# Layer 0 of a four-layer network: how projections are dealt out over attention units, and where small statistics products are written

## The chip, the cores and the metric

The kernel runs on one core of one Trainium2 chip. The time is the device time of one execution in microseconds (us). The core has five engines that run side by side and wait for each other through semaphores: TensorE (PE in the profile, with its weight loads as PEld), VectorE (DVE), ScalarE (ACT), GpSimd (POOL) and SyncE (SP), which here issues nearly all transfers. Everything is computed in 32-bit floats.

## The reference, cut to what matters

Four images of 56 x 56 pixels with 256 channels pass through four layers. Each layer adds something to its input, and normalises its input by groups of 8 channels first:

```python
def _gn(v, G=32, eps=1e-5):                     # per image: mean and variance of each group of 8 channels
    g = v.reshape(B_, H_, W_, G, C_ // G)
    m = jnp.mean(g, axis=(1, 2, 4), keepdims=True)
    s = jnp.var(g, axis=(1, 2, 4), keepdims=True)
    return ((g - m) / jnp.sqrt(s + eps)).reshape(v.shape)

x = x + _L0_conv_ref(_gn(x), ...)               # local attention, 7 x 7 window, 8 heads of 32
x = x + _L1_conv_ref(_gn(x), ...)               # a graph product over the tokens of each image
x = x + _L2_conv_ref(_gn(x), ...)               # neighbourhood attention, 7 x 7, half of the heads dilated by 2
x = x + _L3_conv_ref(_gn(x), ...)               # attention within shifted 7 x 7 windows

def _L0_conv_ref(x, wq, bq, wk, bk, wv, bv, wo, bo):
    q = x @ wq.T + bq; k = x @ wk.T + bk; v = x @ wv.T + bv
    ...                                         # to 8 heads of 32 channels
    k_unf = _unfold(k); v_unf = _unfold(v)      # the 49 neighbours of each pixel, zeros outside the image
    logits = jnp.einsum('ndhw,ndkhw->nkhw', q, k_unf) * scale
    attn = jax.nn.softmax(logits, axis=1)
    out = jnp.einsum('nkhw,ndkhw->ndhw', attn, v_unf)
    ...
    return out @ wo.T + bo
```

The statistics of an image must be complete before the first of its pixels can be normalised. That is what ties the steps around this change together.

## The kernel before, in words

**Units of layer 0.** An image is cut into 8 blocks of 7 rows (`NB0`), and a block into 4 columns (`NTC`) that are 16, 12, 12 and 16 pixels wide. A block and a column make a unit: 32 blocks, 128 units, numbered here through all images. The columns at the sides are wide units (112 queries), the inner ones narrow (84). `pair(r, t)` describes unit t of block r. For each unit there are

- *logits* (L1067): products of queries and keys into two double banks `ps_s`. VectorE adds a mask to the first half (L1074), after which ScalarE takes exp (L1075). ScalarE takes exp of the second half at once (L1077), and GpSimd multiplies that by a mask (L1078);
- *both* (L1087): GpSimd adds pairs of the exps;
- *products* (L1096): the exps times the values and times ones, into one bank `ps_o` (two buffers), the output bank. They fill 448 or 336 of its 512 columns;
- *finish*: VectorE adds a count of outside pixels (L1246), takes the reciprocal (L1249, or L1244 for inner units) and multiplies (L1251), into `attn`. ScalarE reads the reciprocals once for a check (L998).

`attend_pairs` sets the order of the trace: logits of unit u, then the *fill* of unit u, then products and finish of unit u - 1. The fill is a list of other steps, and this is what the change deals out anew.

**What goes into the fills.** An image's input is also cut into 7 chunks of 8 rows (`NCH`). For each chunk, `prepare` has ScalarE normalise it (L942) into `xn`, and `project_rows` makes six steps: values twice (`value_tiles`, L979, drained by VectorE at L983 and stored to DRAM), keys twice and queries twice (`project`, L952, drained by ScalarE at L1202 and L1211). All write banks of `ps_m`, of which there are two. `project_out` makes two steps for the block before (L952 with `w_wo`, drained by VectorE at L1275 into `xr`). `first_look` has VectorE take the statistics of a chunk of the next image (L896), and `load` fetches such a chunk.

**Statistics.** When the last part of an image's statistics is there, `add_stats` appends three steps to `pending`: `channels` (VectorE, L910), `mean` (a product with a group matrix, L914, read by ScalarE at L916 and L917) and `scale` (two products, L921 and L922, read by ScalarE at L923, then small steps on GpSimd from L924 to L928). The products write 2 columns of a whole `ps_m` bank. `step_stats` does the next pending step; `known` does all that is left when somebody needs the result.

**Who sets the order.** `stream` in `layer0` builds each block's list of steps and `spread` cuts it into four equal parts by the number of entries, whatever an entry is. The list holds projection steps, `prepare` as an entry of its own, looks, one entry with loads, the output steps in the middle and, in blocks 0 and 4 to 7 of each image, three `step_stats`. Block r takes projection entries up to `(7 * (7 * r + 12)) // 8`. From block 29 (`ALONE`) the first steps of layer 1 take the place of projections. In layers 0 and 2 a scheduler may still move an instruction ahead on its engine where its inputs are ready; in layers 1 and 3 some engines keep the written order. Layer 2 has units of the same form (`pair` at L1954), filled from a list that is written out by column, with `step_stats` in the columns 1, 4 and 5 of eight.

Of the kernel before, what the change touches and what calls it, by code (L numbers as in the profile page):

```python
# [40 lines left out]
NCH = 7  # L41
# [19 lines left out]
NB0 = S // TR  # L61
BT = TR * S
COLS = (0, 16, 28, 40, 56)
NTC = 4
# [766 lines left out]
def direct_blocks(ctx: ExitStack, tc: tile.TileContext, d: dict, watch):  # L831
# [40 lines left out]
    def psum_tile(tag, bufs, banks=1):  # L872
        shape = [P, 512] if banks == 1 else [P, banks, 512]
        return ps.tile(shape, FP, tag=tag, name="ps_" + tag, bufs=bufs)
# [3 lines left out]
    def ps_m():  # L878
        return psum_tile("m", m_bufs)
# [6 lines left out]

    parts_of = [NCH, NB0, NCH, 2 * NSB]
    raw = [[const.tile([P, CC, n, 6], FP, name=f"st{l}_{b}") for b in range(NIMG)] for l, n in enumerate(parts_of)]
    stats, pending = {}, []
    seen_parts = {}  # L890

    def add_stats(l, b, i, x):
# [8 lines left out]
    def group_stats(l, b):  # L901

        st = raw[l][b]
        mv = const.tile([P, CC, 2], FP, name=f"mv{l}_{b}")
        gst = const.tile([P, CC, 3], FP, name=f"gst{l}_{b}")
        dv = const.tile([P, CC], FP, name=f"dv{l}_{b}")

        def channels():
            for h in range(CC):
                nc.vector.bn_aggr(out=mv[:, h, :], in_=st[:, h].rearrange("p a b -> p (a b)"))  # L910

        def mean():
            pm = ps_m()
            nc.tensor.matmul(pm[:, :CC], lhsT=group, rhs=mv[:, :, 0], start=True, stop=True)  # L914
            for h in range(CC):
                nc.scalar.activation(dv[:, h:h + 1], pm[:, h:h + 1], AF.Square, bias=mv[:, h, 0:1], scale=-1.0)  # L916
            nc.scalar.copy(gst[:, :, 0], pm[:, :CC])  # L917

        def scale():
            pm = ps_m()  # L920
            nc.tensor.matmul(pm[:, :CC], lhsT=group, rhs=dv, start=True, stop=False)  # L921
            nc.tensor.matmul(pm[:, :CC], lhsT=group, rhs=mv[:, :, 1], start=False, stop=True)  # L922
            nc.scalar.activation(dv, pm[:, :CC], AF.Identity, bias=gn_eps)  # L923
            nc.gpsimd.tensor_tensor(gst[:, :, 1], dv, mhalf, ALU.pow)  # L924
            nc.gpsimd.tensor_tensor(gst[:, :, 2], gst[:, :, 0], gst[:, :, 1], ALU.mult)
            nc.gpsimd.tensor_scalar_mul(gst[:, :, 2], gst[:, :, 2], -1.0)
            w = watch[1][:, :2 * CC].rearrange("p (h a) -> p h a", h=CC)
            nc.gpsimd.tensor_tensor(w, w, gst[:, :, :2], ALU.add)  # L928
            stats[l, b] = gst
        return [channels, mean, scale]  # L930
# [119 lines left out]


    newest = []

    def attend_pairs(pool, units):

# [68 lines left out]
    def lazily(make, i, n):  # L1124

        made = []
        return [lambda k=k: (made or made.extend(make(i)), made[k]()) for k in range(n)]
# [7 lines left out]
    def layer0(early, big, pool, begin_layer1):  # L1135
# [10 lines left out]
        def first_look(r):  # L1146

            with tc.issue_after(newest[0].ins) if newest else nullcontext():
                add_stats(0, *divmod(r, NCH), looks.pop(r))
# [36 lines left out]
        def project_rows(r):  # L1186

            b, g = divmod(r, NCH)
            xn = xns.pop(r)
            at = left(g, CH)  # L1190
            v = brief.tile([P, 4, C], FP, tag="v", name="v0", bufs=1)

            def values(a):
                value_tiles(v, a, g, CH, xn, wv, bv0, vd[b])

            def keys(m):
                pm = project(wk, m * P, lambda h: xn[:, h, at:at + CH], CH)
                rows = pm.rearrange("p (r c) -> p r c", c=S)
                for i in range(NTC):
                    c0, n = key_range(*COLS[i:i + 2])  # L1200
                    dst = (kE if i in (0, NTC - 1) else kI)[:, m, i // 2, 8 * g:8 * (g + 1), :]
                    nc.scalar.activation(dst, rows[:, :, c0:c0 + n], AF.Identity, bias=bk0[:, m:m + 1])  # L1202

            def queries(m):
                pm = project(wq, m * P, lambda h: xn[:, h, at:at + CH], CH)
                y = 8 * g
                while y < 8 * (g + 1):
                    i, y1 = y // TR, min((y // TR + 1) * TR, 8 * (g + 1))
                    if (b, i) not in q:
                        q[b, i] = early.tile([P, CC, BT], FP, tag="q", name="q0", bufs=6)  # L1210
                    nc.scalar.activation(q[b, i][:, m, (y - TR * i) * S:(y1 - TR * i) * S],  # L1211
                                         pm[:, (y - 8 * g) * S:(y1 - 8 * g) * S],
                                         AF.Identity, bias=qbias[:, 0, m:m + 1], scale=SCALE)
                    y = y1

            return [lambda f=f, m=m: f(m) for f in (values, keys, queries) for m in range(2)]

        def pair(r, t):

# [8 lines left out]
            box = {}  # L1228

            def gather():  # L1230
                box["o"] = psum_tile("o", 2)
                box["v"] = pool.tile([P, 2, C], FP, tag="vp", name="vp0", bufs=3)
                src = vd[b][:, :]
                for u, k0 in enumerate((0, second)):
                    for p, y, x, rows, cols in row_runs(k0, nk, n):
                        nc.sync.dma_start(out=box["v"][p:p + rows * cols, u, :], in_=bass.AP(
                            src.tensor, src.offset + ((r0 + y) * S + c0 + x) * C, [[S * C, rows], [C, cols], [1, C]]))
# [43 lines left out]
        def stream():  # L1281
            n = NIMG * NCH
            rows = []
            for c in range(2, n):
                rows += lazily(project_rows, c, 6)
                rows.append(lambda c=c: prepare(c + 1) if c + 1 < n else None)
            look_at = {}
            for b in range(NIMG - 1):
                for i in range(NCH):
                    look_at.setdefault(NB0 * b + min(i // 2 + (b == 0), 3), []).append((b + 1) * NCH + i)  # L1290
            gone = 0
            for r in range(NIMG * NB0):
                b, g = divmod(r, NB0)
                to = min(len(rows), (7 * (7 * r + 12)) // 8)
                steps, gone = rows[gone:to], to
                steps += [lambda i=i: first_look(i) for i in sorted(looks)]
                steps.append(lambda r=r: [load(i, looks, "xs") for i in look_at.get(r + 1, [])])
                if 0 < r < ALONE:
                    at = (len(steps) + 2) // 2
                    steps[at:at] = project_out(r - 1)  # L1300
                if g > 3 or g == 0:
                    size = len(steps) + 3
                    for i in range(3):
                        steps.insert(i * size // NTC, step_stats)
                attns[r] = pool.tile([P, CC, BT], FP, tag="attn", name="attn0")
                if r < ALONE:
                    yield from spread([pair(r, t) for t in range(NTC)], steps)
                    continue
                if r == ALONE:
                    passing.close()  # L1310
                    tokens.extend(begin_layer1())
                out = project_out(r - 1)
                for t in range(NTC):
                    w = pair(r, t)
                    w["fill"] = lambda steps=tokens.pop(0) + (out[t - 1:t] if t else []): [f() for f in steps]
                    yield w
# [10 lines left out]
        attend_pairs(pool, stream())  # L1327
        for step in tokens.pop(0) + project_out(NIMG * NB0 - 1):
            step()

# [519 lines left out]
    def layer2(held, big, pool, brief, last_steps, ends):  # L1852
# [64 lines left out]
        def pair(r, m, i):  # L1917
# [23 lines left out]

            def gather():
                box["o"] = psum_tile("o", 2)
                box["v"] = pool.tile([P, 2, 2, P], FP, tag="vp", name="vp2", bufs=3)
                src = vd[im][:, :]
                for t in range(2):
                    c0 = window_range(*cols[t], n)[0]
                    if m == 0:
                        v0, sr, sc = (r0 * S + c0) * C, S * C, C
                    else:  # L1950
                        v0, sr, sc = ((2 * r0 + a) * S + 2 * c0 + b) * C + P, 2 * S * C, 2 * C
                    for u, k0 in enumerate((0, second)):
                        for p, ky, kx, rows, some in row_runs(k0, nk, nc_):
                            nc.sync.dma_start(out=box["v"][p:p + rows * some, t, u, :], in_=bass.AP(  # L1954
                                src.tensor, src.offset + v0 + ky * sr + kx * sc, [[sr, rows], [sc, some], [1, P]]))
# [83 lines left out]
        attend_pairs(pool, stream())  # L2039
        for step in project_out(NIMG * NSB - 1):  # L2040
            step()

# [370 lines left out]
```

## Time and profile before

| what | value |
|---|---|
| median of 3 runs | 3770.52 us (3767.21 to 3772.34) |
| profiled execution, its own time | 3769.93 us |
| its span, first to last instruction | 3768.0 us |
| instructions | 112324 |
| granted TensorE clock, mean | 0.994 |
| layer 0, first logits to last products | 39.8 to about 735 us |
| layer 1 | about 732 to 2600 us |
| layer 2 | about 2600 to 3250 us |
| layer 3 | to 3768 us |

The stage limits are read from TensorE's instructions in order of time. A line of a group or of the timeline names the source line, the engine, the operation and the tiles it writes and reads; "x16" counts instructions, of which a 32-bit product takes two, so a projection step of keys, queries or output has 16 and one of two value tiles 32. Idle time in brackets stands before the instruction, with the instruction whose end released it. PEclk is the granted TensorE clock as a share of full speed.

### The profile page before, as it was taken

To read this page: it belongs to the slowest core of one execution; us is meant where nothing else is said; L and a number is where in the kernel's file an instruction comes from. 1 tells how busy PE (TensorE), PEld (TensorE's weight loads), DVE (VectorE), ACT (ScalarE), POOL (GpSimd) and SP (SyncE) were. 2 spreads that over 40 slices of the span, in tenths; PEclk is the share of its full clock that TensorE was granted. 3 is DMA by queue.
4 is the path that set the end of the run, shared out by engine and by line. 5 is a ranking of instruction groups with operands and counts; after the bars stand their busy time and mean duration, and the time that the engine had idled before them with its cause. 6 is when DMAs were issued, how large, how long until landed. Compare 5 with 4: busy or idle time off the path is not lost. (4 is left out here: it accounts for less than half of the span.)

```text
span 3768.0 us, 112324 instructions
## 1 busy us (share of the span) xinstructions
PE 3665.8 (97%) x48826; PEld 2478.1 (66%) x48826; DVE 2200.9 (58%) x4188; ACT 1472.2 (39%) x3125; POOL 1815.9 (48%) x1966
## 2 busy tenths in 40 slices
PE   8999999999999999999999999999999999999998
PEld 4555556677776777767777667775666666555554
DVE  5777777634445444464344544445676777777676
ACT  5565566422222222222222222222666666444443
POOL 4777777612235222352222421123777777555555
PEclk9999999999999999999999999999999999999999
DMA  6544444300010000011000000002544444534443
GB/s 213 169 153 134 132 123 137 134 7 23 23 27 29 22 19 18 21 32 28 19 16 22 26 20 10 11 20 78 138 133 137 132 128 119 155 126 139 130 134 99
DMA packets 278039, 304.94 MB, mean 81 GB/s; under 512 B 33624, under 2 KB 268764, under 8 KB 277084
## 3 DMA queue, kind: packets, MB, share of 16 engines
q1 hardware_dynamic: 275680, 297.43, 25.7%
q8 instruction: 385, 6.31, 0.7%
q0 software_dynamic: 1568, 0.16, 0.1%
q14 instruction: 118, 0.97, 0.1%
q10 hardware_dynamic: 288, 0.08, 0.0%
HBM read 205.04 MB, written 92.55 MB: 79 GB/s over the span
## 5 line engine op out<-in xcount | busy, mean ns | idle before, releaser
L1564 DVE TENSOR_TENSOR acc<-acc,ps_v 128x257 f32<-128x257 f32 x1104 | 463.8, 422 | 781.8 <-PE ps_v L1642 753.4
L1642 PE MATMUL ps_v<-xw,e 128*128 128x257 f32 x2208 | 611.0, 381 | 3.4 <-DVE xnT L1509 2.2
L1637 PE MATMUL ps_o<-xw,at 128*128 128x257 f32 x2208 | 609.0, 379 | 0.0
L1532 PE MATMUL ps_s<-xnT,xd 128*128 128x512 f32 (+3 forms) x1344 | 571.4, 548 | 3.9 <-DVE xnT L1509 3.9
L1626 ACT COPY at<-ps_t 128x512 f32<-128x512 f32 (+3 forms) x332 | 170.6, 514 | 960.9 <-PE ps_t L1623 960.7
L1642 PEld LDWEIGHTS ps_v<-xw,e 128*128 128x128 f32 x2208 | 413.4, 189 | 144.6 <-issue 83.2
L1087 POOL TENSOR_TENSOR b<-e 126x336 f32<-126x336 f32 (+5 forms) x512 | 499.5, 997 | 7.7
L1637 PEld LDWEIGHTS ps_o<-xw,at 128*128 128x128 f32 x2208 | 419.1, 190 | 60.1
L952 PE MATMUL ps_m<-xn,w_wqkv 128*32 128x392 f32 x4096 | 376.4, 496 | 8.0 <-ACT gst L917 3.4
L1525 POOL TENSOR_SCALAR xd<-xnT,vec 128x128 f32<-128x128 f32 x192 | 116.4, 616 | 478.0 <-PE ps_s L1532 477.8
L1078 POOL TENSOR_TENSOR e<-e,m0t 126x672 f32<-126x672 f32 (+3 forms) x128 | 238.8, 1865 | 182.1 <-ACT e L1077 180.6
L1535 ACT ACTIVATE e<-ps_s 128x512 f32<-128x512 f32 x336 | 185.4, 552 | 355.0 <-PE ps_s L1532 351.8
L1532 PEld LDWEIGHTS ps_s<-xnT,xd 128*128 128x128 f32 x1344 | 225.4, 191 | 141.4 <-issue 126.2
L1078 POOL TENSOR_TENSOR e<-e,bias 119x784 f32<-119x784 f32 (+5 forms) x128 | 239.4, 1870 | 157.3 <-ACT e L1077 156.9
L1096 PEld LDWEIGHTS ps_o<-e,vp 124*32 124x32 f32 (+3 forms) x8192 | 200.3, 110 | 101.9 <-issue 84.1
L998 ACT ACTIVATE no<-rs 128x168 f32<-128x168 f32 (+2 forms) x256 | 94.0, 367 | 426.0 <-DVE rs L1960 190.2
L952 PEld LDWEIGHTS ps_m<-xn,w_wqkv 128*32 128x32 f32 x4096 | 123.8, 110 | 183.1 <-issue 128.6
L1960 DVE RECIPROCAL rs<-ps_o 128x196 f32<-128x196 f32 (+2 forms) x128 | 175.7, 1372 | 109.7 <-PE ps_o L1096 108.0
L1096 PE MATMUL ps_o<-e,vp 124*32 124x112 f32 (+3 forms) x8192 | 232.2, 249 | 3.1 <-POOL e L1078 2.5
L1075 ACT ACTIVATE e<-e 126x672 f32<-126x672 f32 (+5 forms) x256 | 219.7, 858 | 13.3 <-DVE e L1074 1.9
L1077 ACT ACTIVATE e<-ps_s 126x672 f32<-126x672 f32 (+5 forms) x256 | 206.3, 806 | 5.4 <-PE ps_s L1067 3.0
L979 PE MATMUL ps_m<-w_wqkv,xn 128*32 128x256 f32 x3136 | 196.9, 381 | 2.1 <-DVE v L983 1.6
(214 smaller groups left out, 5945.5 us busy)
## 6 DMA issues: line engine op xcount, KB each, us to landing
x<-xr SPq DMA_DIRECT2D x64, 392.0 KB
x<-in_x SPq DMA_DIRECT2D x53, 448.0 KB
x<-x SPq DMA_DIRECT2D x60, 392.0 KB
xr<-x SPq DMA_DIRECT2D x60, 392.0 KB
vd<-v SPq DMA_DIRECT2D x72, 256.0 KB
xr<-in_x SPq DMA_DIRECT2D x32, 392.0 KB
xr<-x SPq DMA_DIRECT2D x28, 448.0 KB
x<-xr SPq DMA_DIRECT2D x28, 448.0 KB
```

What stands on the lines that cost most here:

```text
L952: nc.tensor.matmul(pm[j * HD:(j + 1) * HD, :n], lhsT=w[:, h, col + j * HD:col + (j + 1) * HD], rhs=rhs(h), start=(h == 0), stop=(h == CC - 1))
L979: nc.tensor.matmul(pm[i:i + HD, j * C:(j + 1) * C], lhsT=xn[:, h, first + i:first + i + HD], rhs=w[:, h, :], start=(h == 0), stop=(h == CC ...
L1075: nc.scalar.activation(ev, ev, AF.Exp)
L1077: nc.scalar.activation(ev, sv, AF.Exp)
L1078: nc.gpsimd.tensor_tensor(parts(ev), parts(ev), w["emask"], ALU.mult)
L1087: nc.gpsimd.tensor_tensor(w["b"][a][:nk, :, :2 * nq].rearrange("p h (i c) -> p h i c", i=2), ev[:, :, :, 0, :], ev[:, :, :, 1, :], ALU.add)
L1096: nc.tensor.matmul(w["o"](k, i)[j * HD:(j + 1) * HD], lhsT=ones[:nk, :HD] if k else v(j, u), rhs=w["b"][j // 2][:nk, j % 2, i * nq:(i + 1) ...
L1532: nc.tensor.matmul(s[:, :n], lhsT=xd[j][:, h, :], rhs=xnT[:, h, first * P:last * P], start=(h == 0), stop=(h == CC - 1))
L1535: nc.scalar.activation(e[:, :n], s[:, :n], AF.Exp, scale=5.0)
L1564: nc.vector.tensor_tensor(acc[:, i, :], acc[:, i, :], pv[:, :C + 1], ALU.add)
L1637: nc.tensor.matmul(out[j][:, :C + 1], lhsT=e[:, col(i)] if i == j else at[:, col(i)], rhs=xw[:, i, :], start=(i == j), stop=(i == NB - 1))
L1642: nc.tensor.matmul(pv[:, :C + 1], lhsT=e[:, col(i)], rhs=xw[:, j, :], start=True, stop=True)
```

## The change

In layer 0, the entries of a block fall into two kinds. Products (projection and output steps) are shared out over the four units by their number alone, in the new generator `balanced`. All other steps are assigned to units by hand (`free`): `step_stats` at the head of units 0, 1 and 2, looks in unit 1 (the first two) and unit 2 (the rest), loads in unit 3. `prepare` is tied to the last projection step of a chunk. Block r takes projection entries up to `(6 * (7 * r + 12)) // 8`, six to a chunk. From the third chunk's list on (r of 2 and more) the six steps come as keys, values, queries for the first half and then for the second. Looks at the next image are loaded three chunks to a block (`i // 3`), so that an image's statistics are complete a block earlier, and `step_stats` stands in block 3 as well.

The products of `mean` and `scale` write columns 508 to 511 of the output bank `ps_o` of the unit in which they are traced, where such a bank is at hand (`spare`, set by `gather` in layers 0 and 2 and cleared after them), instead of a bank of `ps_m`.

```diff
+    stats, pending, spare = {}, [], []
...
         def mean():
-            pm = ps_m()
+            pm = spare[0][:, 508:510] if spare else ps_m()
...
         def scale():
-            pm = ps_m()
+            pm = spare[0][:, 510:512] if spare else ps_m()
...
+    def balanced(units, steps, free):
+
+        n = len(units)
+        for i, w in enumerate(units):
+            mine = free[i] + steps[i * len(steps) // n:(i + 1) * len(steps) // n]
+            w["fill"] = lambda mine=mine: [f() for f in mine]
+            yield w
...
-            return [lambda f=f, m=m: f(m) for f in (values, keys, queries) for m in range(2)]
+            kinds = (keys, values, queries)
+            if r < 2:
+                return [lambda f=f, m=m: f(m) for f in (values, keys, queries) for m in range(2)]
+            return [lambda f=f, m=m: f(m) for m in range(2) for f in kinds]
...
                 box["o"] = psum_tile("o", 2)
+                spare[:] = [box["o"]]
...
-                rows += lazily(project_rows, c, 6)
-                rows.append(lambda c=c: prepare(c + 1) if c + 1 < n else None)
+                *most, last = lazily(project_rows, c, 6)
+                rows += most + [lambda c=c, last=last: (last(), prepare(c + 1) if c + 1 < n else None)]
...
-                    look_at.setdefault(NB0 * b + min(i // 2 + (b == 0), 3), []).append((b + 1) * NCH + i)
+                    look_at.setdefault(NB0 * b + i // 3 + (b == 0), []).append((b + 1) * NCH + i)
...
-                to = min(len(rows), (7 * (7 * r + 12)) // 8)
+                to = min(len(rows), (6 * (7 * r + 12)) // 8)
                 steps, gone = rows[gone:to], to
-                steps += [lambda i=i: first_look(i) for i in sorted(looks)]
-                steps.append(lambda r=r: [load(i, looks, "xs") for i in look_at.get(r + 1, [])])
+                new = [lambda i=i: first_look(i) for i in sorted(looks)]
+                free = [[], new[:2], new[2:], [lambda r=r: [load(i, looks, "xs") for i in look_at.get(r + 1, [])]]]
                 if 0 < r < ALONE:
-                    at = (len(steps) + 2) // 2
+                    at = (len(steps) + 1) // 2
                     steps[at:at] = project_out(r - 1)
-                if g > 3 or g == 0:
-                    size = len(steps) + 3
+                if g > 2 or g == 0:
                     for i in range(3):
-                        steps.insert(i * size // NTC, step_stats)
+                        free[i].insert(0, step_stats)
...
-                    yield from spread([pair(r, t) for t in range(NTC)], steps)
+                    yield from balanced([pair(r, t) for t in range(NTC)], steps, free)
...
         for step in tokens.pop(0) + project_out(NIMG * NB0 - 1):
             step()
+        spare.clear()
```

Layer 2 gets the line with `spare[:]` in its `gather` and the line with `spare.clear()` at its end.

More of the change, by code (lines that the diff above doesn't have):

```diff
@@ L888, in direct_blocks @@
     raw = [[const.tile([P, CC, n, 6], FP, name=f"st{l}_{b}") for b in range(NIMG)] for l, n in enumerate(parts_of)]
-    stats, pending = {}, []
+    stats, pending, spare = {}, [], []
     seen_parts = {}
@@ L1943, in gather @@
                 box["o"] = psum_tile("o", 2)
+                spare[:] = [box["o"]]
                 box["v"] = pool.tile([P, 2, 2, P], FP, tag="vp", name="vp2", bufs=3)
@@ L2041, in layer2 @@
             step()
+        spare.clear()
     def table_steps(big, pool):
```

## The prediction, made before the changed kernel ran

> **What bounds the kernel now.** I read the page first, then stretches of layer 0, then who waited for whom, then the order in time.
>
> ```profile
> PE 3665.8 (97%) x48826; PEld 2478.1 (66%) x48826; DVE 2200.9 (58%) x4188; ACT 1472.2 (39%) x3125; POOL 1815.9 (48%) x1966
> PEclk9999999999999999999999999999999999999999
> ```
>
> TensorE is busy for 3665.8 of 3768.0 us, and both kernels issue the same number of instructions on every engine. So only the 102 us in which TensorE stands, and the slow-clock time, can be won. Layer 0 ends near 735 us. The stretches answer has length, then busy time of TensorE first:
>
> ```profile
> 60.00:500.00 440.00, 415.00 (x9469) 257.17 (x9465) 324.38 (x472) 259.45 (x617) 323.02 (x268) 0.99 0.46 144
> 500.00:629.00 129.00, 128.48 (x3076) 81.56 (x3068) 99.49 (x141) 80.71 (x187) 104.47 (x82) 1.00 0.40 125
> ```
>
> The first stands for 25.0 us, the second for 0.5 us. The second holds image 3 (no next image to look at), where every unit happens to have a product. That is the target. The waits of TensorE from 0 to 735 us (total, times, longest) say what ends the standing:
>
> ```profile
> PE ps_s L1067 <- DVE e L1074: 9.8, 11, 1.8
> PE ps_m L979 <- ACT xn L942: 7.0, 3, 2.6
> PE ps_m L952 <- ACT gst L917: 4.8, 4, 1.2
> PE ps_m L952 <- ACT kE L1202: 3.8, 7, 1.1
> PE ps_o L1096 <- POOL b L1087: 2.7, 5, 1.1
> PE ps_m L952 <- ACT dv L923: 1.1, 4, 0.3
> ```
>
> Two places in TensorE's order of time (start, length, instruction; idle time in brackets):
>
> ```profile
> 285.54 0.50 PE L1096 MATMUL ps_o<-b,ones 126*32 126x84 f32 x16 [0.44 <-POOL b L1087]
> 286.72 1.13 PE L1067 MATMUL ps_s<-q,kE 32*124 32x112 f32 x32 [0.69 <-DVE e L1074]
> ...
> 296.97 1.71 PE L952 MATMUL ps_m<-xn,w_wk 128*32 128x448 f32 x16 [1.20 <-ACT gst L917]
> ...
> 311.80 1.13 PE L1067 MATMUL ps_s<-q,kE 32*124 32x112 f32 x32
> 315.10 4.70 PE L979 MATMUL ps_m<-w_wv,xn 128*32 128x256 f32 x48 [2.17 <-ACT xn L942]
> ```
>
> At 285.5 a unit without a projection goes straight from products to logits, and the next logits wait for the mask add (L1074). At 297.0 the third projection since a statistic waits for the bank that its 2-column result holds. At 315.1 statistics of the next image came out at the last moment. After it the clock is at half:
>
> ```profile
> 317.00:319.00 2.00, 2.00 (x24) 1.08 (x20) 0.69 (x1) 2.00 (x4) 0.79 (x1) 0.50 0.84 236
> ```
>
> **What the Trainium skill says.** "TensorE: Matmul & The Clock Gate", Part 1: the clock falls to half when TensorE has been idle for a window of about 3.4 us. The trace agrees in kind, not in size: gaps of 2.17 us were enough (0.50 above), one of 1.75 us at 122.67 was not. The same page, Part 2 ("Step-by-step"): matmuls stay in program order, so a waiting small product holds all that stands behind it; the gap at 297.0 shows that. "PSUM — Partial Sum Buffer", "PSUM bank collisions": two engines may not touch one bank and quadrant at once, other columns included. So a statistic in a unit's output bank must be read by ScalarE before that unit's products are written. No run here shows this yet; in the compiled order those products stand about a unit (5.3 us) later, so I cost it at nothing.
>
> **The change part by part.** "Compiled order" is the engines' order that the scheduler gives; layers 0 and 2 leave it free.
>
> *Even sharing.* Among units 0 to 115 (four columns per block, blocks 0 to 28) nine have no projection before (7, 11, 15, 39, 43, 47, 71, 75, 79) and eleven hold more than two; after, none has none, and only unit 3, in the first block, holds more than two. The last three blocks are shared as before. The nine, and units 35 and 67 with one, are the eleven waits on L1074: 9.8 us go. K, K, Q in a row (waits on kE, 3.8) becomes K, V, Q, so two banks are drained by ScalarE and VectorE in turn: goes. The three waits on POOL's b before 637 us (1.3) and one on v (0.7) follow empty or full units: go. Could one-product units wait anew? From logits' end a one-product unit gives 1.6 (projection) + 1.3 (products) = 2.9 us before the next logits; the mask add is done 2.5 us after it if VectorE is on time. It holds narrowly.
>
> *Looks and statistics earlier.* Looks at the next image come three to a block instead of two, two of them in column 1. VectorE there: finish 2.4, mask 0.85, looks 4 x 0.61 = 2.4, value add 0.7, so 6.4 us against TensorE's 5.9; the next column has 6.3 against 5.1. It falls 1.7 us behind, less than the two units' slack, but near it: I add 0.5 us in each of six blocks, 3.0 (bounds 0 and 9). In return statistics of images 2 and 3 are worked off in blocks 11 to 12 and 19 to 20, without the forced chain: the two 2.17 us gaps go (4.3), and the clock's loss with them. The value products after them took 4.70 and 5.35 us for 48 rows; 56 rows at full clock take 3.43, so 48 take 2.94: 1.8 + 2.4 = 4.2 us go. The extra loads move on SP's queue past gathers; a gather stands a unit ahead of its products, and the value rows it needs are stored several units earlier, so they stay hidden; if not, a gather's landing would show as a wait on vp.
>
> *Spare columns.* The waits on gst and dv (4.8 + 1.1 = 5.9 us, four statistics) go. But the scale step's product (L921) now writes a tile whose buffer is that of two units before, and in the compiled order it waits for that unit's last read, the attn multiply. How long, from a trace of such a unit:
>
> ```profile
> 214.38 0.56 PE L1096 MATMUL ps_o<-b,ones 95*32 95x112 f32 x16
> 214.88 0.88 PE L1067 MATMUL ps_s<-q,kI 32*90 32x84 f32 x32
> 215.09 0.39 DVE L1246 TENSOR_TENSOR rs<-ps_o,outside 128x224 f32<-128x224 f32 x1 [0.53 <-PE ps_o L1096]
> 215.51 1.55 DVE L1249 RECIPROCAL rs<-rs 128x224 f32<-128x224 f32 x1
> 217.10 0.39 DVE L1251 TENSOR_TENSOR attn<-ps_o,rs 128x224 f32<-128x224 f32 x1
> ```
>
> Products end at 214.94, the multiply at 217.49: 2.55 us. TensorE has only the logits to fill this (1.0) and one small projection instruction (about 0.1): it stands 1.45 us. Behind it wait the rest of the projection, then VectorE's add into xr. Six statistics are done so in layer 0: 8.7 us come (bounds 0, if the path is otherwise late there, and 12). The mean step takes the free buffer, without a wait. Layer 2 has four: gst waits 3.4 us go; there the finish is a reciprocal (1.37) and a multiply (0.4) with 0.3 of gaps, so about 2.1 - 1.0 = 1.1 us each come, 4.4. Net +1.0 (bounds -3.4 and +4).
>
> *Tail.* At block 29 the exp of the first unit stood behind layer 1's normals, which waited for a load: TensorE stood 2.53 us and the clock fell (0.50 and 0.70 over 2 us each: 1.6 us lost). In the compiled order the normals now stand behind that exp; the next exp waits for the same load. I take -2.0 (bounds 0 and -4.1).
>
> **Sum.** Gone: 9.8 + 3.8 + 1.3 + 0.7 + 5.9 + 4.3 + 4.2 = 30.0. Then -30.0 + 8.7 + 3.0 + 1.0 - 2.0 = -19.3. Against the profiled execution's 3769.93 (span 3768.0) this is 3750.6; the median of the three runs is 0.6 us higher, 3770.5, so 3751.2. Cross-check: images 1 and 2 take 169.4 and 170.4 us (first logits 203.86, 373.30, 543.66); image 3's blocks 24 to 27, with blocks 12 to 15 freed of their waits and slow clock, would make some 157, about 1.5 us an image more than the listed waits, from gaps too short to be listed. I take a third of that and predict **3750.0**.
>
> **The rivals.**
> - *Waits only move.* VectorE is 74% busy at 60 to 500 us, and looks packed three to a block sit beside the output projection's adds. If each of the six dense blocks pays two waits like 224.11's 1.24 us, that is 15 us instead of 3: -7.5, so 3763. For it: that wait followed exactly such a packed unit. Against: image 3. Chance 13%, a third of it within the bound.
> - *The scale waits cost the clock (slower).* At the ten L921 places, if VectorE is late by 0.5 us, the gap is about 2.0 us and each trips the half clock at up to 2.4 us: 10 x 4.4 = 44. The rest of the sum is -30.0 - 3.4 - 2.0 + 3.0 = -32.4, so +11.6: 3782. It decides from a gap near 2 us, between 1.75 (no fall) and 2.17 (fall). Against: VectorE has no looks in those blocks. Chance 5%.
> - *It gains nothing measurable:* the freed gaps are eaten by POOL (4.4 us in a wide unit) and the new waits: within 7.5 us of 3770. Chance 5%. That the code does otherwise than said is ruled out by the compiled order.
> - *The forecast,* 77%: 3740 to 3760.
>
> **The numbers.** 0.2% (7.5 us) is about what a measurement of this kernel tells from no change. Faster by more: 77 + 9 = 86%; within: 4 + 5 = 9%; slower: 5%. Lower end: without residue and scale waits -30.0 - 3.4 - 4.1 is 3733, unlikely in full, so 3738; the upper end reaches into the first rival, 3763.
>
> **What would show it.** Right: no L1067 waits on L1074 before 637 us; no L979 wait on xn near 315 and 484, the clock at 1.00 there; no waits on gst in layers 0 and 2; instead ten waits of L921 on attn of 1 to 1.5 us; images 1 and 2 at 158 to 161 us. Wrong: L1067 waits after units with looks; half clock after an L921; waits on vp; layer 2 longer by more than 4 us.

## The result, and the profile after

The changed kernel takes **3751.2 us** (median of 6 runs, 3748.4 to 3752.2) against 3770.9 us of the kernel before in the same comparison. The ratio is 0.9948, with a 95% interval of 0.9938 to 0.9958: 19.7 us less, where 3750.0 were forecast. The profiled execution has a span of 3748.2 us against 3768.0.

The page's line of busy times, and then TensorE in two stretches of layer 0 (length, busy PE, PEld, DVE, ACT, POOL, clock, DMA share, GB/s):

```profile
PE 3658.8 (98%) x48826; PEld 2477.5 (66%) x48826; DVE 2203.5 (59%) x4188; ACT 1472.0 (39%) x3125; POOL 1812.2 (48%) x1966
```
```profile
60.00:490.00 430.00, 421.08 (x9780) 266.48 (x9774) 333.71 (x483) 265.88 (x629) 329.90 (x274) 1.00 0.49 150
490.00:617.00 127.00, 125.90 (x2934) 78.70 (x2934) 95.93 (x135) 77.91 (x186) 100.02 (x82) 1.00 0.38 118
```

The first stretch stands for 8.9 us where it stood for 25.0, at full clock. Image 3 (second line) stands for 1.1 us, a little more than before. Who TensorE waited for, in layer 0 (0 to 716 us) and then in layer 2 (2550 to 3235 us), as total, times, longest:

```profile
PE ps_o L921 <- DVE attn L1263: 5.1, 6, 0.9
PE ps_m L952 <- DVE attn L1263: 4.5, 4, 3.8
PE ps_m L952 <- ACT kE L1210: 2.9, 6, 0.8
PE ps_m L979 <- ACT xn L942: 2.6, 1, 2.6
```
```profile
PE ps_o L921 <- ACT no L998: 4.3, 4, 1.2
```

(The changed kernel's lines stand 8 to 13 further down: L1074, L1202 and L1251 of before are L1082, L1210 and L1263.) The eleven waits of L1067 on the mask add are gone, and so are those of L952 on gst and dv. One wait on xn is left, at the kernel's start. In their place stand the ten waits of the scale's product, L921, which were forecast; in layer 2 the trace names ScalarE's read of the reciprocals (L998) as what ended them, not the multiply. The single long wait on attn, 3.8 us, is in the tail (blocks 29 to 31, where layer 1 begins) and was not forecast.

Where the time went, from the starts of logits in the order of time. The last column is the start of layer 1's first small product (L1586, L1574 before), which is used below as **the mark** for the end of layer 0.

| | image 0 | image 1 | image 2 | blocks 24 to 28 | block 29 to the mark | the mark |
|---|---|---|---|---|---|---|
| before | 164.4 | 169.4 | 170.4 | 99.8 | 88.9 | 732.3 |
| after | 160.4 | 161.9 | 162.0 | 100.6 | 89.0 | 713.2 |

All of the gain, 19.1 us at the mark, is in the first three images. From the mark to the first logits of layer 2 both take 1880.4 to 1880.5 us.

### The profile page after: what moved, and what is told of

Its sections match the earlier page's. It is cut to its first block, busy times and chain, and to the rows that moved or that the text cites. A ratio compares the mean times of both kernels' runs of the same rounds, so it can differ in the third digit from the quotient of the medians.

```text
span 3748.2 us, 112333 instructions
## 1 busy us (share of the span) xinstructions
PE 3658.8 (98%) x48826; PEld 2477.5 (66%) x48826; DVE 2203.5 (59%) x4188; ACT 1472.0 (39%) x3125; POOL 1812.2 (48%) x1966
## 5 line engine op out<-in xcount | busy, mean ns | idle before, releaser
L952 PE MATMUL ps_m<-xn,w_wqkv 128*32 128x392 f32 x4096 | 376.9, 497 | 4.6 <-ACT kE L1908 3.2
L1104 PEld LDWEIGHTS ps_o<-e,vp 124*32 124x32 f32 (+3 forms) x8192 | 200.5, 110 | 101.2 <-issue 81.6
L998 ACT ACTIVATE no<-rs 128x168 f32<-128x168 f32 (+2 forms) x256 | 94.0, 367 | 409.8 <-DVE rs L1973 192.2
L952 PEld LDWEIGHTS ps_m<-xn,w_wqkv 128*32 128x32 f32 x4096 | 124.7, 110 | 179.9 <-issue 129.4
L1104 PE MATMUL ps_o<-e,vp 124*32 124x112 f32 (+3 forms) x8192 | 229.8, 248 | 3.5 <-POOL e L1086 2.9
L979 PE MATMUL ps_m<-w_wqkv,xn 128*32 128x256 f32 x3136 | 196.8, 381 | 2.1 <-DVE v L983 1.6
```

The source lines that it names most:

```text
L952: nc.tensor.matmul(pm[j * HD:(j + 1) * HD, :n], lhsT=w[:, h, col + j * HD:col + (j + 1) * HD], rhs=rhs(h), start=(h == 0), stop=(h == CC - 1))
L979: nc.tensor.matmul(pm[i:i + HD, j * C:(j + 1) * C], lhsT=xn[:, h, first + i:first + i + HD], rhs=w[:, h, :], start=(h == 0), stop=(h == CC ...
L1104: nc.tensor.matmul(w["o"](k, i)[j * HD:(j + 1) * HD], lhsT=ones[:nk, :HD] if k else v(j, u), rhs=w["b"][j // 2][:nk, j % 2, i * nq:(i + 1) ...
```

## The experiments

**How they are read.** The mark is the sharper instrument: two executions of the changed kernel put it at 713.23 and 713.01 us. Layer 2 is not: the changed kernel, in two executions, and e5 to e7, which share its layer 2, took 640.5 to 648.5 us from its first logits to layer 3's first value product (L979). Much of that is the granted clock. By the traces' record of it, TensorE was at half clock for 13.7 us of layer 2 in the first of these two executions, for 23.9 in the second and for 3.4 in e5. So differences of a few us are read at the mark, as far as layer 0 is meant. Each mark comes from one execution and contains the tail, from block 29 on, which took 88.5 us in the changed kernel's second execution and 89.0 in its first; differences near 1 us at the mark are therefore not pressed. The ratio compares each kernel with the kernel before in the same comparison.

| kernel | sharing | looks at the next image | products of the statistics | their steps in the fill | time, us | ratio to before, interval | mark |
|---|---|---|---|---|---|---|---|
| before | old | late | ps_m | among the others | - | 1 | 732.3 |
| e2 | old | late | spare | among the others | 3766.3 | 0.9997 (0.9988 to 1.0005) | 728.9 |
| e10 | even | late | ps_m | at the head | 3756.6 | 0.9969 (0.9956 to 0.9981) | 718.2 |
| e1 | even | early | ps_m | at the head | 3757.6 | 0.9971 (0.9960 to 0.9983) | 718.5 |
| e5 | even | late | spare | at the head | 3749.3 | 0.9955 (0.9942 to 0.9969) | 711.9 |
| after | even | early | spare | at the head | 3751.2 | 0.9948 (0.9938 to 0.9958) | 713.2 |
| e3 | even | early | mean spare, scale ps_m | at the head | 3742.1 | 0.9934 (0.9921 to 0.9948) | 711.0 |
| e12 | even | early | ps_m | at the end | 3742.0 | 0.9932 (0.9919 to 0.9946) | 710.2 |
| e11 | even | late | spare | at the end | 3746.0 | 0.9941 (0.9927 to 0.9954) | 710.8 |
| e4 | even | early | spare | at the end | 3740.2 | 0.9923 (0.9909 to 0.9936) | 705.2 |

The kernel before took 3766.8 to 3770.9 us in the four comparisons. The changed kernel, run again beside e10 to e12:

> The changed kernel once more, unaltered, beside the three below on one chip, so that they are compared with it directly. Every theory: 3748 to 3752 us; layer 1's first small product (xdr) within 0.3 us of the 713.2 us of the first trace.

It took 3751.2 us there (ratio 0.9957, 0.9944 to 0.9971), with the mark at 713.0.

### What the spare columns do

e1 is the changed kernel with both products in `ps_m`; e2 is the kernel before with the spare columns:

```diff
 e1:
-            pm = spare[0][:, 508:510] if spare else ps_m()
+            pm = ps_m()
...
-            pm = spare[0][:, 510:512] if spare else ps_m()
+            pm = ps_m()
 e2, on before: the same two lines the other way round, and in layers 0 and 2
+                spare[:] = [box["o"]]
...
+        spare.clear()
```

> The changed kernel, with both small products of every statistic back in a bank of their own of ps_m; the even sharing and the earlier looks stay. Theory (sharing and looks carry the gain; the spare columns trade waits on gst and dv, 5.9 + 3.4 us before, for waits on the attn multiply, 5.1 + 4.3 us): 3750 to 3753 us, waits of L952 on gst back at 4 to 6 us in layer 0, waits of L921 on attn gone. Rival (the spare columns carry a third of the 19.7 us): 3757 us or more.

> The kernel before, with the statistics' small products in the spare columns in layers 0 and 2 and nothing else. Theory: 3769 to 3773 us, as the kernel before; the two gaps of 2.17 us before the value products at 315 and 484 us stay, with the clock at half after them, and L1067 still waits for L1074 about 11 times. Rival (the spare columns carry a third): 3764 us or less.

e1 fell to the rival: the mark is 5.3 us later without the spare columns. e2 lies between the two: 3.4 us at the mark, not to be told from nothing in the whole time. Its two gaps before the value products and its eleven waits on L1074 stayed, as its theory said. About half of its 3.4 us is the clock: the half clock at 483 us lasted 3.4 us where it lasted 6.8 before, and block 21, in which it lies, is 1.6 us shorter. So beside the even sharing the spare columns do gain; alone, little of what they do can be told from chance. The waits of TensorE from 39 to 622 us in e1, and then in the changed kernel, say how:

```profile
PE ps_m L952 <- ACT gst L917: 6.0, 5, 1.2
PE ps_m L952 <- ACT kE L1210: 4.9, 6, 1.5
PE ps_m L952 <- ACT dv L923: 2.6, 6, 0.5
```
```profile
PE ps_o L921 <- DVE attn L1263: 5.1, 6, 0.9
PE ps_m L952 <- ACT kE L1210: 2.9, 6, 0.8
```

In this stretch the kernel before had three waits on gst (3.6 us) and three on dv (0.8). With the even sharing they are five and six. The kE row is the part that a look at small products alone misses. Around a statistic of block 12, TensorE and ScalarE in the order of time in e1:

```profile
291.36 1.52 PE L952 MATMUL ps_m<-attn,w_wo 128*32 128x392 f32 x16 [1.19 <-ACT gst L917]
...
297.54 1.71 PE L952 MATMUL ps_m<-xn,w_wk 128*32 128x448 f32 x16 [0.46 <-ACT dv L923]
...
304.53 1.71 PE L952 MATMUL ps_m<-xn,w_wq 128*32 128x448 f32 x16 [1.50 <-ACT kE L1210]
```
```profile
301.97 1.42 ACT L942 ACTIVATE xn<-x,gst 128x448 f32<-128x448 f32 x2 [3.83 <-POOL gst L926]
```

TensorE first pays for gst and dv. These make the whole chain later: GpSimd's last step (L926) ends at 301.9, ScalarE has stood 3.83 us for it at the normalisation, and the drain of the keys (L1210) is queued behind that. So TensorE pays a third time, 1.50 us, at 304.5. In the changed kernel the first two are replaced by one gap of 0.86. ScalarE stands there nearly as long, 3.66 us, but L926 ends at 300.0, 1.9 us earlier, and the third gap is 0.49.

### What the waits of L921 cost

```diff
 e3:
-            pm = spare[0][:, 510:512] if spare else ps_m()     # in scale() alone
+            pm = ps_m()
 e4:
-            mine = free[i] + steps[i * len(steps) // n:(i + 1) * len(steps) // n]
+            mine = sorted(free[i] + steps[i * len(steps) // n:(i + 1) * len(steps) // n],
+                          key=lambda f: f is step_stats)
...
-                    work[u].insert(0, step_stats)            # layer 2
+                    work[u].append(step_stats)
 e12: both edits of e1, and those of e4
```

> The changed kernel, with only the mean's product in the spare columns (it takes a free buffer) and the scale's product in a bank of ps_m. Theory (the waits of L921 on attn stand on the path: 5.1 us in layer 0, 4.3 in layer 2; what comes instead is a wait on dv of 0.3 us each): 3751 - 9.4 + 3 = 3744 to 3746 us. Rival (those waits only shift when the next unit is ready, because VectorE and GpSimd set the pace in such blocks): 3750 to 3753 us.

> The changed kernel, with each statistic's step at the end of a unit's filling work instead of at its head, in layers 0 and 2: the scale's product then comes 3 us later, after the multiply that it waits for. Theory: no waits of L921 on attn, so 3751 - 9.4 = 3741 to 3744 us. Rival (shift only): 3750 to 3753. Second rival (the statistic's chain now ends later and a projection or a normalise waits for it): 3753 or more, with waits of L979 on xn at the start of an image.

> The changed kernel, with the statistics' steps at the end of the fill, and their products in a bank of ps_m as before the change. Theory (what counts is where in the unit the small products stand; a bank of ps_m is then held while the unit's products of attention run): layer 1 at 704 to 707 us, 3738 to 3742 us. Rival (the spare columns are needed too: the next unit's projection waits for the bank): layer 1 at 709 us or later, 3745 us or more.

e4's theory holds: 3740.2 us, and the mark comes 8.1 us earlier than in the changed kernel, for six waits that the trace lists at 5.1 us in all. The lines show why the list is short of it. A scale's product in block 11, in the changed kernel and then in e4:

```profile
268.74 1.12 PE L1075 MATMUL ps_s<-q,kI 32*126 32x84 f32 x32
...
269.80 0.84 PE L952 MATMUL ps_m<-attn,w_wo 128*32 128x392 f32 x2
...
270.96 0.39 DVE L1263 TENSOR_TENSOR attn<-ps_o,rs 128x224 f32<-128x224 f32 x1
...
271.50 0.35 PE L921 MATMUL ps_o<-dv,group 128*128 128x2 f32 x2 [0.86 <-DVE attn L1263]
```
```profile
263.66 1.71 PE L952 MATMUL ps_m<-xn,w_wq 128*32 128x448 f32 x16
...
264.83 0.39 DVE L1263 TENSOR_TENSOR attn<-ps_o,rs 128x224 f32<-128x224 f32 x1
...
265.19 1.69 PE L952 MATMUL ps_m<-xn,w_wk 128*32 128x448 f32 x16
...
266.81 0.38 PE L921 MATMUL ps_o<-dv,group 128*128 128x2 f32 x2
```

In the changed kernel two instructions of the output projection slip in ahead of L921 and their row shows 0.84 us. Sixteen of the same kind take 1.52, so two take about 0.2; the other 0.65 us is standing time that the row hides. 0.86 + 0.65 is 1.5 us, which is what was forecast for each (1.45), and 8.1 / 6 is 1.35. In e4 the multiply L1263 is done 1.6 us before L921 comes up, and the wait is gone.

e3 passed its number in the whole time, yet not for its reason: the mark moved by 2.2 us only. Block 12 still takes 24.1 us, with other waits:

```profile
293.51 1.71 PE L952 MATMUL ps_m<-xn,w_wk 128*32 128x448 f32 x16 [0.47 <-ACT dv L923]
...
300.49 1.71 PE L952 MATMUL ps_m<-xn,w_wq 128*32 128x448 f32 x16 [1.48 <-ACT kE L1210]
```

The normalisation in the same place held ScalarE for 3.82 us. The other 6.5 us that its profiled execution gained over the changed kernel's were in layer 2. There it was at half clock for 3.4 us against 13.7. If TensorE has work all that time, half clock costs half of the time that it lasts, here up to 5.1 us. Whether e3's edit caused any of it stays open: the time at half clock differs by as much between the changed kernel's own two executions.

e12 shows that place and bank both count (its mark fell to the rival, its whole time to the theory): moved to the end without the spare columns, the steps gain 8.3 us at the mark over e1; with them another 5.0. The two add almost exactly, and the place is worth more than the bank (8.1 and 8.3 us against 5.0 and 5.3). Without the bank L921 waits for another buffer,

```profile
PE ps_m L921 <- ACT q L1219: 3.1, 5, 0.6
```

e8 joins e4's layer 0 with e3's layer 2:

```diff
-            pm = spare[0][:, 510:512] if spare else ps_m()     # scale(), with e4's order in layer 0 alone
+            pm = spare[0][:, 510:512] if spare and l < 2 else ps_m()
```

> Statistics at the end of the fill in layer 0 (there 8.1 us shorter by the traces than the changed kernel), and in layer 2 only the mean in the spare columns, at the head (there 6.5 us shorter). Theory (the two parts add, being in different layers): 3751.2 - 8.1 - 6.5 = 3736 to 3738 us. Rival (the layer 2 gain of the third experiment came from how layer 0 left the queues): 3740 to 3743 us.

It took 3739.7 us (0.9931, 0.9917 to 0.9944), mark 705.2: layer 0's gain as in e4, nothing measurable in layer 2. The theory had added a difference of single executions there, and failed. e4 and e8 both beat the changed kernel, and can't be told apart.

### What the early looks do

```diff
 e5 and e11 (e11 with e4's edits), and e10 with e1's:
-                    look_at.setdefault(NB0 * b + i // 3 + (b == 0), []).append((b + 1) * NCH + i)
+                    look_at.setdefault(NB0 * b + min(i // 2 + (b == 0), 3), []).append((b + 1) * NCH + i)
...
-                if g > 2 or g == 0:
+                if g > 3 or g == 0:
```

> The changed kernel, with the looks at the next image two to a block and the statistics from column 4 on again, as before; the even sharing and the spare columns stay. Theory (the early looks remove the two gaps of 2.17 us and 4.2 us of half clock, and cost 3.0 us in the dense blocks): 3751 + 8.5 - 3.0 = 3756 to 3758 us, with L979 waiting for xn near 312 and 474 us and the clock at half after it. Rival (the even sharing alone makes the statistics early enough): 3748 to 3752 us, no such gap.

> The even sharing alone: late looks, and the small products in a bank of ps_m. Theory (the parts add: the run with late looks began layer 1 at 711.9 us, and without the spare columns the changed kernel lost 5.3 us there): layer 1 at 715 to 718 us, 3755 to 3758 us in all. Rival (without spare columns the chain of statistics forced at an image's start takes two banks, and the gap over 2 us and the half clock are back): layer 1 at 722 us or later, 3761 us or more.

> Late looks, and the statistics' steps at the end of the fill, with the spare columns. Theory (looks are worth 1.3 us, the steps' place 8.1, and they add): layer 1 at 703 to 705 us, 3737 to 3740 us. Rival (with both late the statistics are forced at an image's start, the gap before the first product passes 2 us and the clock falls to half): layer 1 at 709 us or later, 3744 us or more.

e5 fell to the rival: with the old looks the mark is at 711.9, 1.3 us *earlier*, of which 0.5 lie in the tail. The forced chain of statistics is still there where the next image's first chunk is due, but it no longer costs the clock. TensorE at that place in block 13 of e5, and then the stretches around it (the clock is third from the end):

```profile
302.61 0.38 PE L921 MATMUL ps_o<-dv,group 128*128 128x2 f32 x2
...
306.08 1.71 PE L952 MATMUL ps_m<-xn,w_wk 128*32 128x448 f32 x16 [1.52 <-ACT xn L942]
```
```profile
304.00:306.00 2.00, 0.56 (x23) 0.38 (x16) 1.97 (x3) 0.74 (x2) 1.15 (x4) 1.00 0.39 116
306.00:308.00 2.00, 1.92 (x34) 0.94 (x38) 0.19 (x1) 2.00 (x6) 0.00 (x0) 1.00 0.19 32
```

The gap is 1.52 us, not 2.17, and the clock stays at 1.00. e10, with no spare columns, has the same (1.58 us): its theory held to 0.2 us, with the mark at 718.2. So with the even sharing alone the clock's loss is gone at this place. What the early looks win there they lose to their own density: from block 8 to 11 e5 takes 77.5 us, the changed kernel 81.2, in which a statistic's step now falls too; in blocks 12 and 13 it is 45.1 against 42.7.

In e11 the mark is 5.6 us later than in e4 (710.8), and the rival's numbers came, but hardly for its reason. Where the statistics are forced, in blocks 13 and 21, the gaps are 1.55 us at full clock, and images 1 and 2 lose 1.7 us in all. 3.8 of the 5.6 us lie in image 0, whose blocks 4 and 5 take 46.2 us against 40.4. There VectorE stood before the drain of a value product (L983) until an earlier store of values to DRAM had ended, and TensorE stood for the multiply behind it:

```profile
126.83 0.69 DVE L983 TENSOR_TENSOR v<-ps_m,bc 128x512 f32<-128x512 f32 x1 [5.20 <-DMA vd<-v]
...
129.97 2.50 PE L952 MATMUL ps_m<-attn,w_wo 128*32 128x392 f32 x16 [2.78 <-DVE attn L1263]
```

After it the clock is at half. e5 and e10, which have the late looks too, show the same wait of VectorE in block 4, 5.13 and 5.00 us; the changed kernel, e1 and e4, with early looks, do not, and nor does the kernel before, with late looks and the old sharing. Block 4 takes 26.7, 29.9 and 26.6 us in e5, e10 and e11, and 21.8 to 23.4 in the changed kernel, e1 and e4. So much of what the early looks are worth beside the even sharing lies in this store, which neither the prediction nor any theory had named. Why it ends late in the three is not shown.

### The order of kinds, and the tail

```diff
 e6:
-            return [lambda f=f, m=m: f(m) for m in range(2) for f in kinds]
+            return [lambda f=f, m=m: f(m) for f in (values, keys, queries) for m in range(2)]
 e7:
-                    nc.scalar.activation(ev, ev, AF.Exp)
+                    newest.append(nc.scalar.activation(ev, ev, AF.Exp))
...
+        def late_normal(c):
+            with tc.issue_after(newest[0].ins), tc.issue_after(newest[1].ins):   # the unit's mask add and exp
+                normal(c)
... (and late_normal for normal in layer 1's list of first steps)
```

> The changed kernel, with a chunk's projections in the order values, values, keys, keys, queries, queries again, instead of keys, values, queries twice. Theory of the prediction (alternating kinds takes away 3.8 us of waits on kE): 3754 to 3756 us. Rival (waits on kE stood at 2.9 us in the changed kernel against 3.8 before, so the order brings about 1 us): 3750 to 3753 us.

> The changed kernel, with layer 1's normals at the end of layer 0 ordered behind the mask add and the exp of the unit in which they are issued. Theory (VectorE held 3.2 us by the sum of squares that waits for ScalarE, and that for a load, is why the attn multiply came late and TensorE stood 3.8 us at 633.5; the clock's loss after it is about 1.3 us): 3751 - 4 to 5 = 3746 to 3747 us. Rival (the load is late for whoever needs it next, so the wait moves on to the small products of layer 1): 3750 to 3752 us.

e6 took 3750.1 us (0.9955, 0.9941 to 0.9969), mark 713.9. That the order of kinds brings 3.8 us is refuted: K, K, Q has fewer waits on kE (1.4 us) and pays the rest to GpSimd's b (4.2 us). What is left, 0.6 us, is too little to call.

The tail, in the changed kernel: VectorE and TensorE from 628 us, block 29.

```profile
632.88 0.29 DVE L1384 TENSOR_TENSOR sq<-sq 128x128 f32<-128x128 f32 x1 [3.19 <-ACT sq L1383]
...
633.09 0.38 DVE L1263 TENSOR_TENSOR attn<-ps_o,rs 128x224 f32<-128x224 f32 x1
...
633.53 2.84 PE L952 MATMUL ps_m<-attn,w_wo 128*32 128x392 f32 x16 [3.82 <-DVE attn L1263]
```

Before, ScalarE's exp stood behind layer 1's normals. Now VectorE's multiply stands behind their sum of squares (L1384), which waits for ScalarE, and that for the same load. In e7 that multiply passes: block 29 takes 19.4 us, not 24.8. But block 30 takes 28.6, not 24.4, and the mark is at 714.3, 1.1 us later; 3750.2 us in all (0.9957, 0.9944 to 0.9971). The rival held: TensorE now waits for layer 1's own values,

```profile
657.07 2.84 PE L952 MATMUL ps_m<-attn,w_wo 128*32 128x392 f32 x16 [1.64 <-DVE xnT L1412]
```

and is at half clock from 656.5 us on. Whether the load itself could land earlier was not tried.

## Why the prediction was right, and where its steps were not

The sum came out within 1.2 us; four of its steps did not. By way of e10 and e5, the mark moved by -14.1 us for the sharing, by -6.4 for the spare columns, and by +1.3 for the early looks, -19.1 in all. By way of e10 and e1 it is -14.1, +0.3 for the looks and -5.3 for the spare columns; half of the 6.4 is block 4, where e10 and e5 have the wait for the store.

- **Even sharing, step "waits of L1067 on L1074 go" (9.8 us): right.** None is left before block 29; the narrow margin of one-product units held. The sharing as a whole, set down at 15.6 us, brought 14.1 alone (e10), but of other parts: blocks 12, 13, 20 and 21, where the gaps and the half clock were, are 7.7 us shorter in it, and block 4 is 6.1 us longer, with VectorE's wait for the store, TensorE's on v and gst behind it, and half clock after a gap of 2.19.
- **"K, V, Q takes away the waits on kE" (3.8): wrong.** They went from 3.8 to 2.9 us, and e6 shows that the order hardly matters. The waits on kE have a second source, seen in e1 and e3: a normalisation that holds ScalarE for gst.
- **"Looks and statistics earlier" (-8.5 + 3.0): the mechanism was misplaced.** The gaps of 2.17 us and the half clock went, as said, but e10 and e5 show that they go with the sharing alone; the early looks themselves came out at +0.3 to +1.3 us, -5.5 having been set down, although they also do away with the store's wait in block 4. The prediction had not asked which part of the change stood between the forced chain and the next product.
- **"Spare columns" (in layer 0 -5.9 + 8.7 = +2.8): wrong in sign, -5.3 (e1) to -6.4 us (e5 against e10).** The term that came was sized well: 1.45 us a place, against 1.35 in e4. The term that went was read from the kernel before, at 5.9 us for four statistics, and was larger beside the even sharing: 9.1 us in e1's list (gst 6.0 + 0.5, dv 2.6) and 2.0 of the 4.9 on kE. The gap listed beside L921, 0.86, was below the forecast 1.0 to 1.5 only because the row ahead of it hid the rest. That two engines must not meet in one bank and quadrant ("PSUM — Partial Sum Buffer" of the Trainium skill, "PSUM bank collisions") was costed at nothing, and no wait of L1104 for ScalarE's read of a statistic is among the waits of the changed kernel.
- **Layer 2 (+1.0): its waits came in the size that was said** (gst 3.4 gone, L921 4.3 come), though ended by L998, but the sum is less than what that layer varies by, and stays open.
- **Tail (-2.0): wrong, 0.** The stall moved from ScalarE's exp to VectorE's multiply. The prediction had checked what stood behind ScalarE's normals, and not what VectorE does with their result.
- **The dense look blocks (+3.0) and the cross-check** left images 1 and 2 at 161.9 and 162.0 us, just past the 158 to 161 forecast. A third of the cross-check's 3.0 us is 1.0, so its own sum makes 3750.2 rather than 3750.0.

So the errors of the looks (+6.8), the spare columns (-9.2 by the same way), the tail (+2.0) and the sharing (+1.5) cancelled to about 1.2. The forecast's number was better than its working, and that is luck. The rival that would have ended slower did not occur: ten gaps at L921, none followed by a fall. The clock from 60 to 617 us is 1.00 above. The Trainium skill's "TensorE: Matmul & The Clock Gate", Part 1, gives about 3.4 us of idleness for the fall; here it came with listed gaps of 2.17 (before), 2.19 (e10, block 4) and 1.64 us (e7), and not with 2.40 (e5, block 4), 1.75 (before), 1.58 (e10) and 1.52 (e5). So the prediction's bound, a fall somewhere between 1.75 and 2.17 us, does not hold either; the last section shows what does.

## What to carry to other kernels

Put a small product whose operand or buffer comes late behind the unit's large products, not in front of them: here the place was worth 8 us and a bank of its own 5. Price a wait that goes in the arrangement that the change makes, not in that of before, and follow its result on to the engine that stands in order behind it (here GpSimd's chain, ScalarE's normalisation and the next drain). When a stall is shifted off one engine, ask what the next engine in the same chain has queued; in the tail it took the stall over whole.

## What the runs showed of the hardware that was not expected

- **A listed wait can be too short.** A short row ahead of a stalled product is stretched over part of the stall (two products in 0.84 us, where about 0.2 is due), so six listed waits of 5.1 us gave 8.1 us back when they were moved.
- **The length of a single listed gap does not settle whether the clock falls; where it lies does.** The traces keep the granted clock of the whole execution. In each of the fourteen, from 40 us on, all stretches at half clock begin whole multiples of 3.413 us apart and last one or two times that, save the one at the kernel's end. So time can be cut into steps of 3.413 us. e5's gap of 2.40 us (126.53 to 128.93) is shared by two steps, and the clock stays; e11's of 2.78 us (127.19 to 129.97) lies in one, and it falls (length, busy PE first; the clock third from the end):

```profile
124.20:127.61 3.41, 2.33 (x34) 0.93 (x26) 1.80 (x3) 0.00 (x0) 1.59 (x2) 1.00 0.18 62
127.61:131.02 3.41, 2.10 (x49) 1.44 (x53) 2.41 (x4) 2.58 (x9) 1.40 (x1) 1.00 0.42 135
131.02:134.44 3.42, 2.57 (x61) 1.64 (x51) 3.32 (x6) 0.86 (x4) 1.98 (x3) 1.00 0.13 40
```
```profile
126.97:130.38 3.41, 0.63 (x12) 0.26 (x12) 3.34 (x5) 0.89 (x3) 0.00 (x0) 1.00 0.31 97
130.38:133.79 3.41, 3.41 (x38) 1.75 (x34) 1.41 (x3) 2.12 (x7) 3.04 (x3) 0.50 0.19 62
```

  In all fourteen traces, a step at full clock in which TensorE stood for more than 1.9 us (40 steps) was always followed by half clock, and one with less than 0.8 us never. Between these both occur: 1.17 us with a fall before (480.12 to 483.53), 1.57 without in e10 (469.49 to 472.90). In the changed kernel's tail the half clock begins at 630.7 us, inside the gap of 3.82, and lasts to 637.6.
- **One stage repeats to 0.2 us and another doesn't:** the end of layer 0 lay at 713.23 and 713.01 us in two executions of the changed kernel, while its layer 2 took 644.3 and 648.5, with 13.7 and 23.9 us of half clock.
